# Second expert weights kept in SBUF, expert numbers read eight at a time, and row tables cleared at the start

## The chip, the cores and the metric

The kernel runs on one core of one Trainium2 chip, as one program. The metric is the time of the whole program on the device in microseconds (us): the median of several runs. The engines are TensorE (PE, with its weight loads PEld), VectorE (DVE), ScalarE (ACT), GpSimd (POOL) and SyncE (SP), which here does nothing but start transfers. Each engine works through its own list of instructions in order and waits on semaphores. All transfers share 16 DMA engines.

## The reference

The input is x of 8 batches, 512 tokens and 128 features, in fp32. Six steps add to it in turn:

```python
x = x + 0.5 * moe(layernorm(x))     # mixture of experts
x = x + attention(layernorm(x))     # 16 heads of 8, rotary, causal
x = x + 0.5 * moe(layernorm(x))     # the same weights again
x = x + 0.5 * fp6(layernorm(x))     # a 128x128 product on values rounded to 6 bits
x = x + mixer(layernorm(x))         # a gated scan over time and a gated FFN
x = x + 0.5 * fp6(layernorm(x))

def moe(x):                         # 8 experts, each token goes to 2 of them
    logits = x @ router_w + router_b
    scores, idx = top_k(logits, 2);  gates = softmax(scores)
    for expert e:                   # W1[e] 128x512, W2[e] 512x128
        out += c[e] * (relu(x @ W1[e] + b1[e]) @ W2[e] + b2[e])   # c[e]: gate, or 0
```

## The kernel before

**Planning.** The kernel is first written down as a graph of operations (`add`, class `Graph`): for each one its engine and estimated time, what it reads and writes, which buffers it takes, and operations that it must follow (`order`). `Graph.search` plays this through a model of the engines, of the DMA wire and of the buffer slots (`SLOTS`, `CAPS`), chooses an order and, where there is a choice, an engine, and the instructions are then issued in that order. Any changed cost, buffer or dependency therefore gives a new order of the whole program; priorities are the longest estimated way to the end plus a `skew`.

**Mixture of experts.** It runs in groups of batches: stage 0 has the groups of batches 0-1, 2-4 and 5-7, stage 2 (after the attention) has four groups of two. For a group, `moe_front` normalizes (rows `um`), computes logits, ranks every token within its two experts, and gets for each token two places in a table of rows in DRAM. Each expert has a whole number of 128-row tiles there, so a group of two batches has 23 tiles and one of three has 31; unused rows must hold zeros or other finite numbers. `eids` is one row of integers in SBUF: the expert of each tile. GpSimd then scatters the rows, 128 tokens with each indirect DMA, into `rows_in` (L783).

`moe_tiles` goes over pairs of tiles. SyncE, for each tile: reads the tile's expert number from `eids` into a register (L813, with a check of its bounds) and starts a transfer of that expert's whole block of weights into one of six `wx` slots (L814). The block, 1156 numbers for each of 128 partitions, holds W1 (512), W2 (512), b2 (128) and b1 (4). SyncE also loads the pair's rows `xs` (L824). PE turns them (L835), does four products with W1 (`hp`, L846), ACT or DVE adds b1 and clips (`hs`, L858), PE does four products with W2 (`yp`, L867; each product is two matmul instructions), DVE adds b2 (`yo`, L876), which frees the wx slot, and SyncE stores the pair to `rows_out` (L881). `moe_combine` gathers each token's two rows with indirect DMAs on GpSimd (L898) and adds them with their gates (L911).

**Clearing.** `clear_rows` (L467) fills a table with zeros from a tile of 128 x 128 zeros, repeated. There are four tables, one for each group number, used by both stages. Table 0 is cleared on SyncE behind the loads of x; the others are in the list `late`, each ordered behind the scatters of an earlier group. In the same list are the constants of the attention and of the tail (`load_late`): the rotary table, weights, biases, and so on. They were ordered behind the scatters of the second group. `clear_for_attention` has GpSimd clear buffers of the attention, and halve two bias vectors (L512 to L514).

**Attention and tail.** `attention` is a chain of `bursts` of score matmuls (L1018), with a pass over them on DVE (L1070), exponentials on ACT (L1081), a mask on GpSimd (L1089) and products with the values (L1125). Expert tiles of both stages are put between them by the planner. `fp6_weight` prepares the rounded weight, and `tail` does the last three steps for each batch.

Of the kernel before, what the change touches and what calls it, by code (L numbers as in the profile page):

```python
# [15 lines left out]
P = 128  # L16
# [22 lines left out]

E_W1, E_W2, E_B2, E_B1 = 0, NFC * P, 2 * NFC * P, 2 * NFC * P + P  # L40
E_ALL = E_B1 + NFC

SLOTS = {"ps": 8, "g": 34, "pm": 8, "wx": 6, "h": 9, "s": 20}
# [303 lines left out]
def kernel(  # L347
    ctx: ExitStack,
    tc: tile.TileContext,
    x: bass.AP,  # L350
    wexp: bass.AP,
    rw: bass.AP,
    rb: bass.AP,
# [51 lines left out]

    late = []

# [5 lines left out]

    def load_late(b, ap, bulk):
        late.append(lambda after: add(
            dma(0), lambda e: nc.sync.dma_start(out=b.t, in_=ap), w=[b], bulk=bulk, order=[after]))
        return b
# [3 lines left out]

    def const(name, ap, is_late=False):
        b = fixed(name, ap.shape)
        n = 4
        for d in ap.shape:
            n *= d
        return (load_late if is_late else load)(b, ap, n)

# [21 lines left out]
    mhalf = filled("mhalf", [P, GTX], -0.5)  # L450
    zero = filled("zero", [P, P], 0.0)
    ones = filled("ones", [P, P], 1.0)

    n_g = max(len(gs) for gs in GROUPS.values())
    n_0 = len(GROUPS[0])
    rows_in, rows_out = [], []
    for g in range(n_g):
        n = max(tiles_of(len(gs[g])) for gs in GROUPS.values() if g < len(gs)) * TW
        rows_in.append(Buf(None, None, "", dram.tile([n, P], F32, tag=f"rows_in{g}", name=f"rows_in{g}")))
        rows_out.append(Buf(None, None, "", dram.tile([n, P], F32, tag=f"rows_out{g}", name=f"rows_out{g}")))  # L460

    def clear_rows(g, order, skew=0.0):
        t = rows_in[g].t
        n = t.shape[0]
        return add(
            dma(0),
            lambda e: nc.sync.dma_start(  # L467
                out=t.rearrange("(n p) c -> p n c", p=P),
                in_=zero.t.unsqueeze(1).to_broadcast([P, n // P, P]),
            ),  # L470
            r=[zero], w=[rows_in[g]], bulk=n * P * 4, order=order, skew=skew,
        )

    for b in range(2, nb):
        load_x(b)
    sp.append(clear_rows(0, sp[-1:], 1e4))
    for g in range(1, n_g):
        late.append(lambda after, g=g: clear_rows(g, [groups[0, min(g, n_0) - 1]["sent"][-1]]))
    rope_s = const("rope_s", rope, True)
    wattn_s = const("wattn_s", wattn, True)  # L480
    future_s = const("future_s", future, True)
    vec_s = const("vec_s", vecs, True)
    wq8_s = const("wq8_s", wq8, True)
    wmix_s = const("wmix_s", wmix, True)
    wout_s = const("wout_s", wout, True)
    half_bq = fixed("half_bq", [P, P])
    load_late(half_bq, bq.partition_broadcast(P), P * P * 4)
    half_vec = fixed("half_vec", [P, 2])
# [5 lines left out]
    def clear_for_attention(after):  # L494
        for h in range(2):
            for k in range(2):
                t = nstat[h][k]
                add(pool(S, each=1e-3), lambda e, t=t: nc.gpsimd.memset(t.t, 0.0), w=[t], order=[after])
        for v in vpad:
            for q in range(4):  # L500
                part = v.t[:, 16 * q : 16 * q + 16, :]
                add(pool(S, each=1e-3), lambda e, part=part: nc.gpsimd.memset(part, 0.0),
                    w=[(v, ("clear", q))], order=[after])
            v5 = v.t.rearrange("p (a two) c -> p a two c", two=2)
            for k in range(2):
                at = 16 * k + DK
                add(pool(32, each=1e-3),
                    lambda e, v5=v5, k=k, at=at: nc.gpsimd.memset(v5[:, :, k, at : at + 1], 1.0),
                    w=[v], order=[after])

        def halves(e):
            nc.gpsimd.tensor_scalar_mul(half_bq.t, half_bq.t, 0.5)  # L512
            nc.gpsimd.tensor_scalar_mul(half_vec.t[:, 0:1], vec_s.t[:, V_BG : V_BG + 1], 0.5)
            nc.gpsimd.tensor_scalar_mul(half_vec.t[:, 1:2], vec_s.t[:, V_BD : V_BD + 1], 0.5)  # L514

        add(pool(P, k=2, each=1.3e-3), halves, r=[vec_s], w=[half_bq, half_vec], order=[after])
# [112 lines left out]
    def moe_front(s, g):  # L629
# [4 lines left out]
        n_b = len(bs)  # L634
        GT, NTL = n_b * NT, tiles_of(n_b)
        n8 = GT * NE
# [140 lines left out]
        for n in range(n_b):  # L777
            for k in range(2):
                for t in range(NT):
                    i = n * NT + t  # L780

                    def scatter(e, n=n, k=k, t=t, i=i):
                        ins = nc.gpsimd.indirect_dma_start(  # L783
                            out=rows_in[g].t[0 : NTL * TW, :],
                            out_offset=bass.IndirectOffsetOnAxis(ap=at(k)[:, i : i + 1], axis=0),
                            in_=tokens(us[n])[:, t, :], in_offset=None,
                            bounds_check=NTL * TW - 1, oob_is_err=False,
                        )
                        state["scattered"].append(unordered(ins, f"out{name}"))

                    state["sent"].append(add(
                        ("POOL", 1.02, 2.2, None), scatter, r=[us[n], (keep, f"at{k}"), (rows_in[g], ("s", name, i, k))],
                        bulk=P * P * 4,
                    ))

    def moe_tiles(s, g):

        NTL = tiles_of(len(GROUPS[s][g]))
        state = groups[s, g]
        for j in range((NTL + 1) // 2):  # L800
            tiles = [i for i in (2 * j, 2 * j + 1) if i < NTL]
            w = len(tiles)
# [6 lines left out]
            for i in tiles:  # L809
                wx[i] = buf("wx", "wx", f"wx_{name}")  # L810

                def fetch(e, i=i, wxi=wx[i]):
                    r = nc.sync.value_load(state["eids"].t[0:1, i : i + 1], min_val=0, max_val=NE - 1)  # L813
                    nc.sync.dma_start(  # L814
                        out=wxi.t, in_=wexp[bass.ds(r, 1), :, :].rearrange("o p c -> p (o c)")
                    )

                loads.append(add(
                    ("SP", 0.73, 3.0, None), fetch, r=[state["eids"]], w=[wx[i]], acq=[wx[i]],
                    bulk=P * E_ALL * 4, order=loads[-1:],  # L820
                ))

            def rows_of(e, xs=xs, rows=rows, halves=halves):
                ins = nc.sync.dma_start(  # L824
                    out=halves(xs.t), in_=rows_in[g].t[rows, :].rearrange("(h p) c -> p h c", p=P)
                )
                data_from(ins, state["scattered"])

            rows_loads.append(add(
                dma(0), rows_of, w=[xs], acq=[xs], deps=state["sent"], bulk=w * P * P * 4, order=rows_loads[-1:]  # L830
            ))

# [30 lines left out]
            for h, i in enumerate(tiles):  # L863

                def second(e, h=h, i=i, yp=yp, hs=hs, wx=wx):
                    for fc in range(NFC):
                        nc.tensor.matmul(  # L867
                            yp.t[:, ts(h, P)], hs[i].t[:, ts(fc, P)],
                            wx[i].t[:, E_W2 + fc * P : E_W2 + (fc + 1) * P],
                            start=(fc == 0), stop=(fc == NFC - 1),  # L870
                        )

                add(pe(P, NFC), second, r=[hs[i], wx[i]], w=[(yp, h)], acq=[yp, yo] if h == 0 else [])

# [5 lines left out]
            def store(e, yo=yo, rows=rows, halves=halves):  # L880
                state["stored"].append(nc.sync.dma_start(  # L881
                    out=rows_out[g].t[rows, :].rearrange("(h p) c -> p h c", p=P), in_=halves(yo.t)
                ))

            state["done"].append(add(dma(0), store, r=[yo], bulk=w * P * P * 4))

    def moe_combine(s, g):

        state = groups[s, g]
        NTL = tiles_of(len(GROUPS[s][g]))  # L890
        for n, b in enumerate(GROUPS[s][g]):
            for k in range(2):
                y = buf("g", "y", f"y{k}_{s}_{b}")
                for t in range(NT):
                    i = n * NT + t

                    def gather(e, y=y, k=k, t=t, i=i):
                        ins = nc.gpsimd.indirect_dma_start(  # L898
                            out=tokens(y)[:, t, :], out_offset=None,
                            in_=rows_out[g].t[0 : NTL * TW, :],  # L900
                            in_offset=bass.IndirectOffsetOnAxis(ap=state["at"](k)[:, i : i + 1], axis=0),
# [3 lines left out]

                    add(("POOL", 1.02, 2.2, None), gather, r=[(state["keep"], f"at{k}")], w=[(y, t)],
                        acq=[y] if t == 0 else [], deps=state["done"], bulk=P * P * 4)
# [452 lines left out]
    for g in range(n_0):  # L1360
        moe_front(0, g)
        if g + 1 < n_0:
            late.pop(0)(None)
    for go in late:
        go(groups[0, 1]["sent"][-1])
    clear_for_attention(groups[0, 0]["sent"][-1])
# [3 lines left out]
    bursts = attention()  # L1370
    fp6_weight(bursts[0])
    for g in range(len(GROUPS[2])):
# [91 lines left out]
```

## Time and profile before

| | |
|---|---|
| median of 3 runs | 1101.2 us (1100.86 to 1102.36) |
| profiled execution: its own time, its span | 1096.83 us, 1095.1 us |
| granted TensorE clock, mean | 0.932 |
| busy: PE, DVE, POOL, ACT | 929.3, 752.4, 536.1, 515.3 us |
| moved by DMA | 163.6 MB, of it wx 177 transfers of 578 KB |
| first scatter, first row load, first expert matmul | 28.57, 51.68, 55.11 us |
| the expert tiles' second matmuls, L867 | 1416 instructions, 199.1 us |

The profile is of one execution. The expert tiles of stage 0 begin at 55 us, alone at first and from about 180 us on between the bursts of the attention, which ends at about 757 us. The first weight load of stage 2 is issued at 488.8 us, and its last tile ends at about 935 us; from there on the tail is alone. In the rows, L numbers are lines of the kernel before. The groups of section 5 give busy time, mean duration and idle time before it; windows give busy times of each engine in a stretch. "issue" is time in which the engine waited for nothing that the profile shows.

### The profile page before, as it was taken

To read this page: it belongs to the slowest core of one execution; us is meant where nothing else is said; L and a number is where in the kernel's file an instruction comes from. 1 tells how busy PE (TensorE), PEld (TensorE's weight loads), DVE (VectorE), ACT (ScalarE), POOL (GpSimd) and SP (SyncE) were. 2 spreads that over 40 slices of the span, in tenths; PEclk is the share of its full clock that TensorE was granted. 3 is DMA by queue.
4 is the path that set the end of the run, shared out by engine and by line. 5 is a ranking of instruction groups with operands and counts; after the bars stand their busy time and mean duration, and the time that the engine had idled before them with its cause. 6 is when DMAs were issued, how large, how long until landed. Compare 5 with 4: busy or idle time off the path is not lost.

```text
span 1095.1 us, 22590 instructions
## 1 busy us (share of the span) xinstructions
PE 929.3 (85%) x7282; PEld 694.7 (63%) x7282; DVE 752.4 (69%) x2797; ACT 515.3 (47%) x1335; POOL 536.1 (49%) x681
## 2 busy tenths in 40 slices
PE   5357958799899989998999999998978989976873
PEld 5357946677667764554765776666877878535452
DVE  7501216278866579997786667966338859999996
ACT  3123523235465654555755665564435536543521
POOL 2771053525722168447246223784048654774552
PEclk9978968799999998999998999999989989988985
DMA  4737969487455411015233354233978876100001
GB/s 147 261 113 250 384 196 331 132 297 225 132 191 158 145 56 50 26 36 182 64 117 100 107 155 141 76 122 93 303 266 270 264 245 214 30 17 1 20 19 39
DMA packets 102070, 163.60 MB, mean 149 GB/s; under 512 B 11200, under 2 KB 70720, under 8 KB 101952
## 3 DMA queue, kind: packets, MB, share of 16 engines
q1 hardware_dynamic: 93760, 145.37, 41.1%
q0 software_dynamic: 8192, 16.79, 5.1%
q8 instruction: 58, 0.95, 0.3%
q14 instruction: 60, 0.49, 0.1%
HBM read 129.28 MB, written 29.16 MB: 145 GB/s over the span
## 4 chain that ended last, share of the span: by engine, by line
PE 50%; DVE 21%; issue 10%; POOL 8%; DMA 6%; another core or an unknown queue 2%; ACT 1%; SPq 1%; POOLq 0%; DVEq 0%; ACTq 0%
PE hp L846 11%; PE yp L867 10%; PE sb L1018 8%; PE sa L1018 7%; PE av L1125 5%; DMA wx<-in_wexp 3%; DVE sa L1070 3%; POOL y L898 3%; POOL rows_in L783 1%; PE xp L835 1%; PE lp L663 1%; DMA y<-rows_out,keep 1%; DVE q L1226 1%; DVE x L911 1%
## 5 line engine op out<-in xcount | busy, mean ns | idle before, releaser
L858 ACT ACTIVATE hs<-hp,wx 128x128 f32<-128x128 f32 x704 | 199.5, 372 | 231.0 <-PE hp L846 115.4
L1070 DVE CUSTOM_DVE_ANT_0 sa<-sa,future_s 128x384 f32<-128x384 f32 (+3 forms) x512 | 241.1, 514 | 86.6 <-PE sa L1018 50.8
L867 PE MATMUL yp<-wx,hs 128*128 128x128 f32 x1416 | 199.1, 287 | 56.3 <-issue 30.2
L1081 ACT ACTIVATE pm<-sb 128x512 f32<-128x512 f32 x320 | 173.3, 598 | 147.5 <-PE sb L1018 67.3
L867 PEld LDWEIGHTS yp<-wx,hs 128*128 128x128 f32 x1416 | 180.7, 200 | 67.8 <-issue 53.6
L846 PE MATMUL hp<-xt,wx 128*128 128x128 f32 x1416 | 200.5, 289 | 9.2 <-DMA wx<-in_wexp 5.1
L1018 PE MATMUL sb<-qa,ka 32*128 32x256 f32 (+3 forms) x1024 | 198.0, 467 | 10.3 <-DVE nstat L1070 6.8
L846 PEld LDWEIGHTS hp<-xt,wx 128*128 128x128 f32 x1416 | 183.1, 202 | 31.4 <-issue 11.8
L1089 POOL TENSOR_SCALAR_AFFINE_SELECT pm<-pm 128x256 f32<-128x256 f32 x256 | 104.3, 426 | 199.2 <-ACT pm L1081 196.6
L1018 PE MATMUL sa<-ka,qm 32*128 32x384 f32 (+3 forms) x1024 | 191.9, 474 | 4.2 <-DVE qm L537 2.4
L898 POOL DMA_INDIRECT y<-rows_out,keep x128 | 136.2, 1064 | 89.7 <-PE yp L867 47.9
L783 POOL DMA_INDIRECT rows_in<-um,keep x128 | 128.7, 1005 | 70.4 <-DVE route L751 32.9
L876 DVE TENSOR_TENSOR yo<-yp,wx 128x128 f32<-128x128 f32 x177 | 48.7, 285 | 124.1 <-PE yp L867 65.3
L1018 PEld LDWEIGHTS sb<-qa,ka 32*128 32x128 f32 x1024 | 98.3, 186 | 49.2 <-DVE nstat L1070 16.7
L1018 PEld LDWEIGHTS sa<-ka,qm 32*128 32x128 f32 x1024 | 88.3, 189 | 31.7 <-issue 7.9
L1125 PE MATMUL av<-pm,vpad 128*32 128x256 f32 (+3 forms) x1024 | 80.4, 445 | 1.8 <-POOL pm L1089 1.3
L535 DVE COPY xt<-xp 128x256 f32<-128x256 f32 (+1 forms) x83 | 33.8, 408 | 59.2 <-PE xp L835 27.4
L1070 DVE DVE_READ_ACCUMULATOR2_ANT nstat<- 128x1 f32 x512 | 72.0, 141 | 0.0
L1125 PEld LDWEIGHTS av<-pm,vpad 128*32 128x32 f32 x1024 | 28.7, 111 | 59.2 <-issue 41.1
L911 DVE SCALAR_TENSOR_TENSOR x<-y,keep,x 128x128 f32<-128x128 f32 x128 | 45.3, 368 | 20.6 <-DMA y<-rows_out,keep 18.6
L835 PE MATMUL xp<-cst,xs 128*128 128x128 f32 x177 | 36.3, 287 | 12.5 <-DMA xs<-rows_in 12.0
L835 PEld LDWEIGHTS xp<-cst,xs 128*128 128x128 f32 x177 | 22.6, 148 | 17.3 <-issue 14.6
(215 smaller groups left out, 1233.6 us busy)
## 6 DMA issues: line engine op xcount, KB each, us to landing
wx<-in_wexp SPq DMA_DIRECT2D x177, 578.0 KB
xs<-rows_in SPq DMA_DIRECT2D x85, 128.0 KB
rows_out<-yo SPq DMA_DIRECT2D x85, 128.0 KB
rows_in<-zero SPq DMA_DIRECT2D x2, 1984.0 KB
rows_in<-zero SPq DMA_DIRECT2D x2, 1472.0 KB
x<-in_x SPq DMA_DIRECT2D x8, 256.0 KB
rows_in<-um,keep POOLq DMA_INDIRECT x128
y<-rows_out,keep POOLq DMA_INDIRECT x128
```

Source lines behind the costliest of these rows:

```text
L783: ins = nc.gpsimd.indirect_dma_start(out=rows_in[g].t[0 : NTL * TW, :], out_offset=bass.IndirectOffsetOnAxis(ap=at(k)[:, i : i + 1], axis= ...
L835: nc.tensor.transpose(xp.t[:, ts(h, P)], halves(xs.t)[:, h, :], ident)
L846: nc.tensor.matmul(hp.t[:, ts(fc, P)], wx[i].t[:, E_W1 + fc * P : E_W1 + (fc + 1) * P], xt.t[:, ts(h, P)], start=True, stop=True,)
L858: nc.scalar.activation(o, a, AF.Relu, bias=bias)
L867: nc.tensor.matmul(yp.t[:, ts(h, P)], hs[i].t[:, ts(fc, P)], wx[i].t[:, E_W2 + fc * P : E_W2 + (fc + 1) * P], start=(fc == 0), stop=(fc == ...
L898: ins = nc.gpsimd.indirect_dma_start(out=tokens(y)[:, t, :], out_offset=None, in_=rows_out[g].t[0 : NTL * TW, :], in_offset=bass.IndirectO ...
L911: nc.vector.scalar_tensor_tensor(X[b].t[:, t, :], tokens(y)[:, t, :], state["gates"](k)[:, i : i + 1], X[b].t[:, t, :], ALU.mult, ALU.add,)
L1018: nc.tensor.matmul(sc.t[:, at : at + hi - lo], stat.t[rows, ts(m, P)], mov.t[rows, lo:hi], start=True, stop=True,)
L1070: nc.vector.tensor_tensor_reduce(out=sc.t[:, at : at + wd], in0=sc.t[:, at : at + wd], in1=future_s.t[:, S - wd : S], scale=-1.0, scalar=3 ...
L1081: nc.scalar.activation(pm.t[:, (h % 2) * S : (h % 2 + 1) * S], sc.t, AF.Exp, scale=scale)
L1089: nc.gpsimd.affine_select(out=diag, in_=diag, pattern=[[0, 2], [1, P]], compare_op=ALU.is_ge, fill=0.0, base=0, channel_multiplier=-1,)
L1125: nc.tensor.matmul(av.t[32 * j : 32 * j + 32, m * P :], v.t[:, row, :], pm.t[:, at : at + S - m * P], start=first, stop=last,)
```

## The change

1. **Weights.** W2 leaves the block `wexp`, whose rows now have 644 numbers. All eight experts' W2 come as one array `wsec` into a resident SBUF tile `w2_s` (128 x 4096 numbers), in two loads right behind the clears. The second matmuls take their right operand from `w2_s` at a place that a register of PE gives.
2. **Expert numbers.** Reads are for eight tiles at a time, without a check of bounds: SyncE reads them for its weight loads, and PE reads them too, for the places in `w2_s`. The planner is told 0.6 us for a read on SP, 0.3 on PE and 0.52 for a weight load (0.73 before). A read on PE comes after the fourth last second matmul before it.
3. **Tables.** Three tables instead of four: the last group of stage 2 uses table 0 again, with dependencies for it. All three are cleared at the start, from a tile of 128 x 1024 zeros that takes a slot of the attention's `pm` buffers, with longer runs.
4. **Constants.** `late` is split: what the attention needs is ordered behind the first group's scatters, what the tail needs (and the halving, and `fp6_weight`) behind a burst of the attention, number 20.

```diff
-E_W1, E_W2, E_B2, E_B1 = 0, NFC * P, 2 * NFC * P, 2 * NFC * P + P
+E_W1, E_B2, E_B1 = 0, NFC * P, NFC * P + P
 E_ALL = E_B1 + NFC
+W2 = NFC * P
+REGS = 8
...
-    zero = filled("zero", [P, P], 0.0)
...
+    table = lambda s, g: g if g < n_0 else 0
...
+    zero = buf("pm", "pm", "zero")
+    add(pool(2 * S, each=1e-3), lambda e: nc.gpsimd.memset(zero.t, 0.0), w=[zero], acq=[zero], skew=9e3)
+    for g in range(n_0):
         t = rows_in[g].t
         n = t.shape[0]
-        return add(
+        sp.append(add(
             dma(0),
-            lambda e: nc.sync.dma_start(
-                out=t.rearrange("(n p) c -> p n c", p=P),
-                in_=zero.t.unsqueeze(1).to_broadcast([P, n // P, P]),
+            lambda e, t=t, n=n: nc.sync.dma_start(
+                out=t.rearrange("(p n) c -> p (n c)", p=P).rearrange("p (q c) -> p q c", q=4),
+                in_=zero.t[:, 0 : n // 4].unsqueeze(1).to_broadcast([P, 4, n // 4]),
             ),
...
-    sp.append(clear_rows(0, sp[-1:], 1e4))
-    for g in range(1, n_g):
-        late.append(lambda after, g=g: clear_rows(g, [groups[0, min(g, n_0) - 1]["sent"][-1]]))
...
+    w2_s = fixed("w2_s", [P, NE * W2])
+    for q in range(2):
+        half = slice(q * NE * W2 // 2, (q + 1) * NE * W2 // 2)
+        load((w2_s, q), wsec[:, half], P * NE * W2 * 2, to=w2_s.t[:, half])
...
+        def registers(engine, to, at):
+            to.update(zip(at, nc.values_load_multi_w_load_instructions(
+                state["eids"].t[0:1, at[0] : at[-1] + 1], engines=[engine], min_val=0, max_val=NE - 1,
+                skip_runtime_bounds_check_because="the tile's expert is held below NE",
+            )[1]))
+
         for j in range((NTL + 1) // 2):
+            if (2 * j) % REGS == 0:
+                at = list(range(2 * j, min(2 * j + REGS, NTL)))
+                loads.append(add(
+                    ("SP", 0.6, 0.6, None), lambda e, at=at: registers(mybir.EngineType.SP, expert, at),
+                    r=[state["eids"]], order=loads[-1:],
+                ))
+                o = add(("PE", 0.3, 0.0, "F"), lambda e, at=at: registers(mybir.EngineType.PE, which, at),
+                        r=[state["eids"]], order=seconds[-4:-3])
+                ready.update({i: o for i in at})
...
-                    r = nc.sync.value_load(state["eids"].t[0:1, i : i + 1], min_val=0, max_val=NE - 1)
                     nc.sync.dma_start(
-                        out=wxi.t, in_=wexp[bass.ds(r, 1), :, :].rearrange("o p c -> p (o c)")
+                        out=wxi.t, in_=wexp[bass.ds(expert[i], 1), :, :].rearrange("o p c -> p (o c)")
                     )
...
                             yp.t[:, ts(h, P)], hs[i].t[:, ts(fc, P)],
-                            wx[i].t[:, E_W2 + fc * P : E_W2 + (fc + 1) * P],
+                            w2_s.t[:, bass.ds(which[i] * W2 + fc * P, P)],
...
+    for go in late["attention"]:
+        go(groups[0, 0]["sent"][-1])
...
-    fp6_weight(bursts[0])
+    for go in late["tail"]:
+        go(bursts[2 * HALF])
+    halve(bursts[2 * HALF])
+    fp6_weight(bursts[2 * HALF])
```

## The prediction

> **What bounds the kernel now.** I read the page first: busy shares, the slices, the chain that ended last.
>
> ```profile
> PE 929.3 (85%) x7282; PEld 694.7 (63%) x7282; DVE 752.4 (69%) x2797; ACT 515.3 (47%) x1335; POOL 536.1 (49%) x681
> ...
> PEclk9978968799999998999998999999989989988985
> DMA  4737969487455411015233354233978876100001
> ...
> PE 50%; DVE 21%; issue 10%; POOL 8%; DMA 6%; another core or an unknown queue 2%; ACT 1%; SPq 1%; POOLq 0%; DVEq 0%; ACTq 0%
> ```
>
> TensorE works 85% of the span, so the sum is made against its 166 us of idle time. DMA is 6% of the chain and SyncE 1% (11 us). DMA slices of 8 and 9 stand in expert stages only. Next, windows cut by stage; the first pair of numbers behind the window's length is PE's busy time, the last three are granted clock, DMA share and GB/s.
>
> ```profile
> 55.00:90.00 35.00, 16.98 (x102) 15.88 (x102) 2.13 (x7) 6.84 (x24) 24.85 (x29) 0.75 0.32 99
> 90.00:135.00 45.00, 42.91 (x364) 42.22 (x365) 11.01 (x37) 23.40 (x84) 0.89 (x1) 0.97 0.99 361
> 135.00:160.00 25.00, 11.70 (x69) 10.82 (x68) 2.08 (x8) 4.56 (x16) 15.11 (x16) 0.69 0.61 206
> 160.00:220.00 60.00, 50.04 (x299) 41.56 (x299) 26.07 (x91) 21.45 (x69) 24.42 (x28) 0.82 0.72 232
> ...
> 757.00:800.00 43.00, 37.84 (x327) 36.85 (x328) 20.16 (x84) 19.30 (x67) 5.03 (x5) 1.00 0.92 299
> ...
> 820.00:900.00 80.00, 70.09 (x513) 62.07 (x512) 59.33 (x207) 40.43 (x122) 54.47 (x50) 0.95 0.81 257
> ...
> 940.00:1095.00 155.00, 107.17 (x458) 69.74 (x458) 143.20 (x403) 58.47 (x126) 87.32 (x75) 0.83 0.06 21
> ```
>
> Two things are to be seen. Where DMA is full (90 to 135, 757 to 800) PE is nearly full too: 95% and 88%. Where PE is bad (55 to 90 at 49%, 135 to 160 at 47%) DMA is at 0.32 and 0.61 and GpSimd is busy 71% and 60%: bursts of scatters and gathers, at a granted clock of 0.75 and 0.69. From 940 on VectorE does 143 of 155 us and the change touches nothing. Third, the chain of waits inside 757 to 800, with the weight loads on it:
>
> ```profile
> 761.00 5.07 DMA wx<-in_wexp
> ...
> 769.65 5.42 DMA wx<-in_wexp
> ...
> 778.76 5.47 DMA wx<-in_wexp
> ...
> 787.57 6.35 DMA wx<-in_wexp
> ```
>
> That is 22.3 of 43 us on the chain, yet PE idles only 5.2 us there: it does other tiles while a load flies. Last, the two lines that read an expert's number and use it on SyncE (duration in ns, min/median/max):
>
> ```profile
> L813 SPq TENSOR_LOAD <-eid x177: 15/272/867, 27.0 to 918.7; - x177
> L813 SPq FUSED_REGOPS  x177: 13/152/181, 27.5 to 919.0; - x177
> L813 SPq SEQ_ASSERT  x177: 8/18/378, 27.7 to 919.2; - x177
> ```
>
> ```profile
> L814 SPq FUSED_REGOPS  x177: 3/37/705, 27.8 to 919.3; - x177
> L814 SPq MOVE wx<-in_wexp x177: 3/29/697, 27.9 to 919.4; - x177
> ```
>
> **The base.** The profiled execution took 1096.8 us (span 1095.1 and 1.7 around it), 4.4 under the median of 1101.2. The terms are differences and are set on the median. About 0.2% (2.2 us) is what a measurement of this kernel can tell from no change.
>
> **Part 1, second weights resident.** A tile's wx shrinks from 578 to 322 KB: 256 KB by 177 tiles is 46.4 MB less of 163.6, for 2 MB loaded once. At the 361 GB/s of 90 to 135 that is 129 us of wire time, but only PE's idle time beside a full wire can come back. Low end: PE sat 5.1 us, in 7 waits, directly behind wx. High end: all PE idle time in the three full stages, 45 - 42.91 = 2.1, 43 - 37.84 = 5.2 and 80 - 70.09 = 9.9, together 17.2. I take the first two whole and half of the third, where GpSimd also bursts (54 of 80 us): 12 us gained. What is late next is PE itself: a tile has 8 + 8 matmuls of L846 and L867, eight of which start within 0.89 us in the timeline (111 ns each), plus a turned half, about 1.9 us, as long as 720 KB of traffic takes at 361 GB/s (2.0 us).
>
> **Part 2, numbers read eight at once.** SyncE: L813 costs 272 + 152 + 18 = 442 ns a tile, 78 us in all. Now there are 23 reads (3 for each of five groups of 23 tiles, 4 for each of two of 31), with no check of bounds. The same thread issues row loads and stores, which thus wait less. At most the chain's 11 us of SyncE goes, at least nothing; I take 2 gained, since the queue waits 248 us for VectorE to free a weight slot, which the change leaves.
>
> TensorE gets two new things. Reads: 23, on the engine that is the bound, and what is queued behind a read are the matmuls of all stages, attention's too. No row shows a read on PE nor one of eight numbers. From SyncE's 272 ns, one read for a batch is 23 x 0.272 = 6.3 us, and a price for each number is 177 x 0.272 = 48. I take one price for a batch, half of it behind matmuls already queued: 3 lost. Zero is the end below; nothing in a read can gain. [...]
>
> Addresses: the right operand of L867 comes through a register, 4 places a tile, 708 in all. The nearest row is SyncE's 37 + 29 = 66 ns for one address: 46.7 us if PE waits for each, 0 if all are made ahead. Four addresses are 0.26 us against the 0.89 us in which the array does the tile's eight second matmuls, so I take them as hidden but for half of a tile's first: 177 x 0.033 = 6 lost. The cover is matmuls in the queue; without it the 46.7 stand. [...]
>
> **Part 3, tables cleared first.** Three tables (1472 + 2 x 1984 = 5440 KB) instead of four (6912). SyncE issues them and the two halves of the resident weights right behind the x loads: 5 issues instead of 1, about 2 us more on a thread that stands from 7.1 to 27.9. The wire is at a share of 0.19 from 12 to 28 us; 5.4 + 2 MB at 361 GB/s take 21 us, to about 33, then six loads of 322 KB to about 39. The first matmul waits for xs, which lands at 53.8 behind 16 scatters: 15 us of cover. The wide zero is one memset of 1.1 us (twice the 565 ns of L502) while GpSimd is idle to 6.1. All this is nothing on the path. What goes are two clears in mid-run (issued at 167.0 and 249.6), 5.6 and 4.2 us of wire ahead of row loads: between 0 and 9.8; PE is 94% and 100% busy in those 20 us windows, so I take 1 gained.
>
> The clear that held the third group's scatters is gone, so their 24 x 1.28 = 31 us may move from 184-209 into the 48 us (86 to 134) in which GpSimd is idle. Bounds: 10 gained (PE's idle time from 160 to 220), or PE runs at 49% as from 55 to 90 instead of 95%, 14 lost. I take 0. The tail's constants and their halving go into the attention; the first user is at 707 us, so nothing. Table 0 serves the first and the last group, some 500 us apart: nothing.
>
> **Sum.** -12 - 2 - 1 + 3 + 6 + 0 = -6: 1090.8 in the profile's terms, 1095 as a median.
>
> **Rivals.** Registers on PE decide (slower): reads and addresses stand in TensorE's order uncovered. The point is where a tile's extra PE time passes the idle time beside it; PE idles under 10% in the stages that matter. Half of 46.7 plus half of 48 is 47, plus nothing else; less the 15 gained, 1133; with one read price a batch and half the addresses, 1101 + 23 + 6 - 15 = 1115. I set it at 1118. For it: PE is 85% busy and every instruction on it delays all stages. Against it: 111 ns a matmul leaves room for 66 ns an address.
>
> Scatters meet full tiles (slower): the third group's burst falls under 90 to 135 and costs 14, the freed time of 160 to 220 is filled by waits for gathers: 1101 + 14 - 6 = 1109. For it: 49% against 95%. Against it: the planner may spread them.
>
> More comes back: 17 for the wire, 10 for the scatters, 3 for SyncE and the clears, 9 lost: 1080. For it: weight loads on the chain. Against it: PE's idle time hardly stands beside them.
>
> It does nothing: traffic was hidden anyway, gains of 9 meet losses of 9: 1101.
>
> **How the numbers follow.** Forecast (1088 to 1099) 0.38; more comes back 0.13; nothing 0.10; registers 0.25; scatters 0.14. Hence faster 0.50 (0.01 of the forecast's weight is within 0.2%), same 0.11, slower 0.39. The forecast's own range is 1088 to 1099; eight in ten need part of the cases of both signs: 1074 to 1124, left out the far half of the register case and the deep end of the gain.
>
> **What would show it.** Right: wx near 322 KB, DMA share from 90 to 135 and 757 to 800 near 0.6 with PE at 97%; the spacing of L867's matmuls still 111 ns; 23 reads on PE under 0.5 us. Wrong: gaps put down to "issue" or PE's queue ahead of the second matmuls; reads of 1.6 us or more; clears landing after 40 us; a new stretch at half PE under GpSimd's scatters between 86 and 134.

## The result, and the profile after

The changed kernel is slower: 1136.65 us in the median (1130.82 to 1139.28, 6 runs) against 1101.62 us (1096.33 to 1102.97, 6 runs) for the kernel before. The ratio is 1.0321, 95% interval 1.0287 to 1.0354, so +35 us where the prediction had -6. Times differ with the chip that a program ran on: the kernel before takes about 1102 us on some (called a slow chip below; this comparison is on one) and about 1021 us on others (a fast chip), so each ratio below is against the kernel before on the same chip. The profiled execution took 1134.79 us (span 1133.1). In the rows below, L numbers are lines of the changed kernel: `hp` is L870 (L846 before), `yp` L891 (L867), the reads of numbers L811, the weight load L838, the scatters L790, the gathers L923.

First the page of the changed kernel: busy times, granted clock and DMA share over 40 slices, and the chain that ended last.

```profile
PE 955.6 (84%) x7282; PEld 705.8 (62%) x7282; DVE 739.1 (65%) x2780; ACT 525.4 (46%) x1357; POOL 537.6 (47%) x682
...
PEclk9995989988999998889999999999975998799995
DMA  9541766732423310021222233314754771000001
...
PE 51%; DVE 19%; DMA 9%; issue 8%; another core or an unknown queue 5%; ACT 4%; POOL 3%; SPq 1%; POOLq 0%; DVEq 0%; ACTq 0%
```

The transfers did become lighter (117.82 MB instead of 163.60, each wx load 322 KB), and still DMA holds more of the chain, 9% instead of 6. PE has the same 7282 matmuls and only 26 us more of busy time. Now the windows that the prediction showed, of the changed kernel. PE's busy time is the first pair behind the length, VectorE's the third, GpSimd's the fifth.

```profile
55.00:90.00 35.00, 25.00 (x170) 22.80 (x171) 3.78 (x11) 11.40 (x40) 29.31 (x38) 0.92 0.46 137
90.00:135.00 45.00, 24.88 (x168) 22.98 (x169) 5.77 (x18) 12.32 (x44) 12.98 (x14) 0.69 0.45 131
135.00:160.00 25.00, 19.95 (x169) 19.07 (x168) 5.32 (x17) 8.79 (x32) 10.18 (x11) 0.98 0.68 190
160.00:220.00 60.00, 50.65 (x377) 47.97 (x377) 18.53 (x70) 28.15 (x98) 15.03 (x15) 0.89 0.69 189
757.00:800.00 43.00, 39.59 (x367) 33.01 (x367) 23.09 (x86) 22.00 (x66) 15.98 (x25) 1.00 0.48 129
820.00:900.00 80.00, 61.66 (x417) 57.18 (x418) 30.77 (x111) 26.95 (x96) 36.23 (x36) 0.79 0.58 161
```

The half-PE stretch that the prediction named as a wrong sign is there: 24.88 of 45 us from 90 to 135, where PE worked 95% before. But it is given back: the bad windows on both sides got better. The row to stop at is 820 to 900. VectorE does 30.77 us where it did 59.33. That work has to go somewhere, so the next windows are cut at the last gather of the last group, which starts at 974.0 us before and 980.2 after. First the kernel before, the stage ahead of it and the rest; then the changed kernel.

```profile
845.00:974.00 129.00, 116.91 (x756) 93.65 (x754) 108.08 (x371) 69.72 (x192) 82.11 (x74) 0.96 0.54 171
974.00:1095.10 121.10, 78.03 (x337) 53.03 (x336) 111.19 (x293) 38.11 (x82) 59.05 (x49) 0.78 0.05 19
```

```profile
860.00:980.20 120.20, 99.66 (x658) 83.15 (x658) 85.41 (x314) 60.41 (x179) 65.31 (x60) 0.87 0.49 137
980.20:1133.10 152.90, 114.59 (x502) 71.41 (x500) 141.06 (x400) 59.81 (x123) 71.22 (x59) 0.86 0.04 15
```

Here stand 31.8 of the 38.0 us between the two spans: behind the last gather VectorE has 400 instructions instead of 293, and the stretch is 152.9 us instead of 121.1. All are steps of the last three layers (the tail) that used to be placed between the expert tiles. The change edits none of these steps. Up to the last gather the changed kernel is only 6.2 us late: the attention's last score matmuls start 15.7 us later (763.3 instead of 747.6), and from there to the last gather, with less tail work between the tiles, it takes 9.5 less.

Last the new instructions, with duration in ns (min/median/max):

```profile
L811 SPq TENSOR_LOAD <-eid x23: 71/529/952, 26.5 to 917.3; - x23
L811 PEldq TENSOR_LOAD <-eid x23: 588/635/1146, 26.5 to 929.2; - x23
```

```profile
L891 PE MATMUL yp<-w_s,hs x1416: 269/275/582, 61.7 to 941.4; 128*128 x177
L891 PEldq FUSED_REGOPS  x708: 51/55/60, 59.3 to 940.0; - x177
```

A read of eight costs TensorE's queue 635 ns, an address 55 ns, four addresses a tile as predicted.

### The profile page after: what moved, and what is told of

The parts are those of the page before. It is cut to its first block, busy times and chain, and to the rows that moved or that the text cites. A ratio compares the mean times of both kernels' runs of the same rounds, so it can differ in the third digit from the quotient of the medians.

```text
span 1133.1 us, 22841 instructions
## 1 busy us (share of the span) xinstructions
PE 955.6 (84%) x7282; PEld 705.8 (62%) x7282; DVE 739.1 (65%) x2780; ACT 525.4 (46%) x1357; POOL 537.6 (47%) x682
## 2 busy tenths in 40 slices
DMA packets 90054, 117.82 MB, mean 104 GB/s; under 512 B 11216, under 2 KB 56912, under 8 KB 89680
## 4 chain that ended last, share of the span: by engine, by line
PE 51%; DVE 19%; DMA 9%; issue 8%; another core or an unknown queue 5%; ACT 4%; POOL 3%; SPq 1%; POOLq 0%; DVEq 0%; ACTq 0%
PE hp L870 12%; PE yp L891 11%; PE sb L1043 8%; PE sa L1043 6%; DMA wx<-in_wexp 6%; PE av L1150 5%; DVE sa L1095 3%; DMA y<-rows_out,keep 2%; PE xp L859 1%; PE lp L670 1%; DVE mix L1362 1%; ACT pm L1106 1%; POOL y L923 1%; PE gt L1356 1%
## 5 line engine op out<-in xcount | busy, mean ns | idle before, releaser
L882 ACT ACTIVATE hs<-hp,wx 128x128 f32<-128x128 f32 x692 | 195.1, 374 | 231.5 <-PE hp L870 106.0
L870 PE MATMUL hp<-xt,wx 128*128 128x128 f32 x1416 | 209.6, 294 | 46.5 <-DMA wx<-in_wexp 26.7
L870 PEld LDWEIGHTS hp<-xt,wx 128*128 128x128 f32 x1416 | 185.3, 204 | 64.4 <-issue 32.8
L891 PE MATMUL yp<-w_s,hs 128*128 x1416 | 198.3, 286 | 21.0 <-issue 18.5
L1043 PE MATMUL sb<-qa,ka 32*128 32x128 f32 (+3 forms) x1024 | 201.2, 476 | 9.7 <-ACT pm L1106 6.1
L1043 PE MATMUL sa<-ka,qm 32*128 32x384 f32 (+3 forms) x1024 | 194.3, 482 | 6.0 <-DVE nstat L1095 4.7
L891 PEld LDWEIGHTS yp<-w_s,hs 128*128 128x128 f32 x1416 | 181.5, 201 | 28.5 <-issue 24.4
L923 POOL DMA_INDIRECT y<-rows_out,keep x128 | 135.0, 1054 | 104.4 <-DMA wx<-in_wexp 66.0
L790 POOL DMA_INDIRECT rows_in<-um,keep x128 | 127.6, 997 | 38.2 <-issue 30.0
L1043 PEld LDWEIGHTS sb<-qa,ka 32*128 32x128 f32 x1024 | 100.8, 189 | 48.7 <-DVE nstat L1095 13.6
L1150 PE MATMUL av<-pm,vpad 128*32 128x256 f32 (+3 forms) x1024 | 83.6, 457 | 0.7 <-POOL pm L1114 0.5
```

Source lines behind the costliest of these rows:

```text
L790: ins = nc.gpsimd.indirect_dma_start(out=rows_in[tb].t[0 : NTL * TW, :], out_offset=bass.IndirectOffsetOnAxis(ap=at(k)[:, i : i + 1], axis=0),
L870: nc.tensor.matmul(hp.t[:, ts(fc, P)], wx[i].t[:, E_W1 + fc * P : E_W1 + (fc + 1) * P], xt.t[:, ts(h, P)], start=True, stop=True,)
L882: nc.scalar.activation(o, a, AF.Relu, bias=bias)
L891: nc.tensor.matmul(yp.t[:, ts(h, P)], hs[i].t[:, ts(fc, P)], w2_s.t[:, bass.ds(which[i] * W2 + fc * P, P)], start=(fc == 0), stop=(fc == N ...
L923: ins = nc.gpsimd.indirect_dma_start(out=tokens(y)[:, t, :], out_offset=None, in_=rows_out[tb].t[0 : NTL * TW, :], in_offset=bass.Indirect ...
L1043: nc.tensor.matmul(sc.t[:, at : at + hi - lo], stat.t[rows, ts(m, P)], mov.t[rows, lo:hi], start=True, stop=True,)
```

## The experiments

Three theories stood at the start. **Order theory:** the planner, given new costs, writes another order for the whole program, and that order costs the time. **Instruction theory:** TensorE's reads and addresses cost it (the prediction's first rival). **Table theory:** the clears and what they free cost it.

The figures of plans in the expectations are what the kernel's own planner computes for its order. The expectations in us for x1 to x4 were meant for a slow chip; to be set beside the results they are read as ratios to 1101.6 us.

**Old and new instructions in each other's order.** The planner's call is replaced by a fixed list of steps, with engine and buffer of each; the list is the one that the planner makes for the other kernel, with steps that only one kernel has put right before their first use.

```diff
-    order = G.search(bursts, SLOTS)
+    order = pinned(G)      # the other kernel's order
```

New instructions, old order (x1):

> All of the changed kernel's instructions (small weight blocks, resident second weights, register reads of eight on SyncE and TensorE, three tables cleared first), but every step put on the engine, at the place and in the buffer that the planner chose for the kernel before; the register reads stand right in front of their first use. Order theory (what costs 35 us is the new order that the planner makes from its changed costs): 1085 to 1102 us, no slower than before. Instruction theory (reads and addresses on TensorE cost it): 1125 to 1140, as the changed kernel. Table theory (clears first, shared table 0): 1115 to 1140 if it is the clears' transfers, 1100 if it is only what they let the planner do.

Old instructions, new order (x2):

> The reverse: full weight blocks of 578 KB, one read of the expert's number for each tile on SyncE, nothing on TensorE, in the order that the planner chose for the changed kernel; tables and clears as in the changed kernel. Order theory: 1130 to 1150 us, as slow as the changed kernel or slower, since 46 MB more have to pass in an order that was made for less. Instruction theory: 1095 to 1105. Table theory: 1125 to 1140.

Measured on a fast chip: x1 0.9907 (0.9873 to 0.9941), x2 1.0751 (1.0694 to 1.0807). Both stand with the order theory, for which x1 was expected at 0.985 to 1.000 and x2 at 1.026 to 1.044 or more: the same instructions gain 9.5 us in the old order, and the old ones lose 77 us in the new one without any instruction of part 1 or 2. The windows behind the last gather show the same fingerprint as the first two profiles, x1 first, then x2.

```profile
891.60:1012.60 121.00, 78.63 (x337) 53.12 (x336) 111.27 (x293) 38.10 (x82) 58.99 (x49) 0.79 0.05 19
```

```profile
944.70:1098.60 153.90, 114.06 (x501) 72.13 (x499) 141.63 (x403) 59.62 (x122) 71.45 (x59) 0.85 0.04 15
```

VectorE's 293 and about 400 instructions, 121 and 153 us, go with the order and not with the instructions. x2 shows one thing more, in its chain: full blocks in an order made for small ones wait for the wire, and DMA has 20% of the chain (9% in the changed kernel).

```profile
PE 43%; DVE 21%; DMA 20%; issue 5%; ACT 4%; POOL 4%; SPq 2%; POOLq 0%; DVEq 0%; ACTq 0%
```

**Single parts, each planned anew.** x3 is the kernel before with parts 1 and 2, x4 the kernel before with part 3.

> The kernel before with the resident second weights and the reads of eight, its four tables, clears and constants as they were; the planner makes its own order. Instruction theory: 1125 to 1140 us. Table theory: 1085 to 1100. Order theory: no fixed number, since it is a third order; near 1100 if the third group's scatters stay behind a clear in mid-run and that is what counts, up to 1140 if any new order is as bad.

> The kernel before with the third part of the change alone: three tables cleared first from the wide zero tile, constants loaded for the attention and for the tail apart; full weight blocks and one read for each tile. The planner makes its own order, with the third group's scatters free to move up. Table theory: 1120 to 1140 us. Instruction theory: 1095 to 1105. Order theory: 1110 to 1140 if the moved scatters are what costs.

On the fast chip x3 took 1.0378 (1.0322 to 1.0435), with 155.9 us behind the last gather; x4 1.0016 (0.9982 to 1.0049), with 121.5 us, though its third group's scatters run from 84 to 114 us instead of behind the first group's gathers. So the table theory falls, and the bad order comes with parts 1 and 2. The stretches of x3 and x4:

```profile
905.10:1061.00 155.90, 115.06 (x502) 73.45 (x500) 141.20 (x403) 57.56 (x119) 72.32 (x59) 0.84 0.04 15
```

```profile
902.10:1023.60 121.50, 77.29 (x337) 52.12 (x336) 111.45 (x293) 38.05 (x82) 59.00 (x49) 0.78 0.05 19
```

**One number of the planner.** Of what parts 1 and 2 tell the planner, the size of a weight load is the largest change. Two kernels change that number and no instruction; two more are the changed kernel itself and a neighbour of its order.

```diff
 # y2, in the changed kernel: what the planner is told of a load that moves 322 KB
-                    bulk=P * E_ALL * 4, order=loads[-1:],
+                    bulk=P * (E_ALL + W2) * 4, order=loads[-1:],
 # y3, in the kernel before: what it is told of a load that moves 578 KB
-                    bulk=P * E_ALL * 4, order=loads[-1:],
+                    bulk=P * (E_ALL - NFC * P) * 4, order=loads[-1:],
 # y4, in the changed kernel
-MIX = 0.2
+MIX = 0.25
```

> The changed kernel as it is, beside the kernel before on the chip of the other runs of this call (one kernel differed by some 80 us between two chips, so the comparison has to be made on one). Order theory: 1.03 to 1.05 of the time before, with the last gather some 155 us before the end as in its first profile, against 121 us in the kernel before. Instruction theory: the same ratio, but then the gap must not close in the two runs that change one number of the planner.

> The changed kernel with one number different: the planner is told that a weight load moves 578 KB, as before, while it moves 322. Its plan then ends the last gather 99 us before the end (126 in the changed kernel's plan), with 72 us of the last layer's VectorE work behind it (88). Order theory: 0.985 to 1.005 of the time before, last gather to end 120 to 125 us. Instruction theory: 1.03 or more, as the changed kernel, since every instruction is there.

> The kernel before with one number different: the planner is told that a weight load moves 322 KB, while it moves 578. No instruction is changed, only the order. Its plan has the last gather 127 us before the end and 89 us of the last layer's VectorE work behind it (98 and 70 before). Order theory: 1.04 to 1.08 of the time before, last gather to end about 155 us. Instruction theory and table theory: 1.00.

> The changed kernel with the planner's mixing of old and new priorities at 0.25 instead of 0.2: another order from the same costs, whose plan ends the last gather 126 us before the end too. If the loss comes from the costs that the planner is given: 1.03 to 1.06 of the time before, last gather to end about 155 us. If the loss is the luck of one order: anywhere from 0.98 to 1.06, and not tied to that stretch.

On one fast chip: y1 1.025 (1.0175 to 1.0325), y2 1.0004 (0.9969 to 1.0039), y3 1.061 (1.0539 to 1.0682), y4 1.0217 (1.0152 to 1.0283). Telling the old size takes the loss away with every new instruction in place; telling the new size to the kernel before makes it 6% slower with not one instruction changed. y4, a neighbouring order, is as bad, with 149.8 us behind the last gather. y1 and y4 both came out a little below the 1.03 expected at least. The stretches of y1, y2 and y3:

```profile
890.70:1045.00 154.30, 115.17 (x502) 72.92 (x500) 141.09 (x400) 59.94 (x123) 71.27 (x59) 0.87 0.04 15
```

```profile
894.10:1016.90 122.80, 82.73 (x347) 54.27 (x345) 112.07 (x304) 42.55 (x92) 60.33 (x50) 0.79 0.05 19
```

```profile
936.10:1086.40 150.30, 114.21 (x502) 71.58 (x500) 138.93 (x403) 59.95 (x127) 73.49 (x60) 0.87 0.04 16
```

The first numbers are to be read too: the last gather starts at 890.7 us in y1, 894.1 in y2, and 891.6 in x1. The plan of the changed kernel has it some 40 us earlier than the plan of before (808 instead of 849); on the chip the order that put 30 us of VectorE's work behind it was no earlier at all. y1 and y2 ran on one chip and reach it within 3.4 us of each other; from there on y1 takes 31.5 us longer.

**The terms of the sum, in the old order.** z1 is x1 without TensorE's reads and chosen addresses (each tile takes a fixed block, so its output is another one); z2 has full blocks, no resident tile and nothing on TensorE. p1 and p2 repeat z1 and x1 side by side, x5 repeats x1 alone.

```diff
 # z1 and p1, against x1
-                            w2_s.t[:, bass.ds(which[i] * W2 + fc * P, P)],
+                            w2_s.t[:, i % NE * W2 + fc * P : i % NE * W2 + (fc + 1) * P],
 # and the read on PE issues nothing; z2, against that
-                            w2_s.t[:, i % NE * W2 + fc * P : i % NE * W2 + (fc + 1) * P],
+                            wx[i].t[:, E_W2 + fc * P : E_W2 + (fc + 1) * P],
```

> The kernel of x1_new_ops_old_order (new instructions, old order) without TensorE's part of the numbers: no register reads on TensorE, and the second matmul takes the resident block of tile number modulo 8 at a fixed address instead of the chosen expert's (so its output is another one). It prices the two TensorE terms of the prediction, +3 and +6 us. If they are as predicted: 9 us faster than x1, ratio 0.982. If the address arithmetic is hidden and only the 23 reads show: 0.984 to 0.991. If TensorE's registers cost nothing: 0.991, as x1. [...]

> Old order, full weight blocks of 578 KB with the second weights in them, nothing on TensorE; from the change only SyncE's reads of eight, and the three tables cleared first. Against z1 it prices the wire term alone (-12 us predicted), against the kernel before SyncE's reads and the clears (-3 predicted). If the terms are right: 0.997 of before, z1 being 12 us faster. If the wire is worth nothing in this order: 0.98 to 0.99, equal to z1. If the wire is worth more: z2 at 1.00 and z1 at 0.975.

> The new instructions in the old order once more, as x1: 0.985 to 0.995 on any chip, if the sum of the prediction (-6 us) is right about the instructions. On a chip of the slow kind, against z1's 0.988 there: 0.991 if TensorE's reads and addresses cost the 2 to 3 us that x1 and z1 differ by, 0.997 if they cost the 9 predicted.

> z1 once more (old order, new instructions, without TensorE's reads and chosen addresses, the second matmul on a fixed block), now beside the full one on one chip. If the terms are as predicted (9 us): 0.8 per cent under the full one. If they are hidden: equal. If the difference between the calls was real (15 us): 1.3 per cent under.

> New instructions, old order, complete (as x1 and x5), beside p1. 0.99 of before on a chip of the fast kind, 0.99 to 1.00 on one of the slow kind; above p1 by 0 (hidden), 9 us (predicted) or 15 us (the difference between the calls).

All on slow chips: z2 0.9970 (0.9941 to 1.0000); z1 0.9884 (0.9848 to 0.9921), p1 0.9893 (0.9855 to 0.9931); x5 1.0019 (0.9979 to 1.0060), p2 1.0024 (0.9998 to 1.0050). Differences of ratios times 1102 us give the terms, with the half widths put together as a root of squares: SyncE's reads and the clears -3.3 us (0 to -6.5); the wire, z1 less z2, -9.5 (-4 to -15); TensorE's numbers, p2 less p1, +14 (+9 to +20). x5 and p2 lie above what was expected of them (at most 0.997 and 1.00 on a slow chip), which fits a last term larger than thought. The middle one can be seen in part in PE's idle time before the first matmuls (z2 first, then z1): the waits for wx go away, 4.3 us of them.

```profile
L861 PE MATMUL hp<-xt,wx 128*128 128x128 f32 x1416 | 202.1, 290 | 6.8 <-DMA wx<-in_wexp 4.3 <-ACT pm L1096 0.9 <-DVE route L684 0.7
```

```profile
L870 PE MATMUL hp<-xt,wx 128*128 128x128 f32 x1416 | 199.9, 288 | 2.8 <-issue 2.8
```

How TensorE's numbers cost 14 us is not settled. The middle spacing of the second matmuls is 112 ns in p1 and in p2 alike, and there is no gap ahead of a tile's first one that one has and the other has not (median 111 to 112 ns in both). The 23 reads fill 18 us of PE's queue in x5's profile, which is of the right size, yet where no indirect DMA runs they hold up no matmul. Set side by side matmul by matmul, p2's profile is 6.89 us behind p1's at 310 us and still 6.89 at 395 us, with two reads and 21 tiles' second matmuls in between; it is 3.30 behind at 611 and 3.29 at 684, with one read and 15 tiles. The lag, 8.5 us at the end of these two profiles, is built up where GpSimd issues indirect DMAs; how is open. No run kept the reads and left out the addresses. On a fast chip x1 was at 0.9907, so it may cost less there; that was not paired.

**How far the told size carries.** The size of y2, raised to 640 and 720 KB:

> The changed kernel's instructions, the planner told that a weight load moves 640 KB (it moves 322). The plan leaves 62.9 us of the last layer's VectorE work behind the last gather (88.5 in the changed kernel's plan, 71.6 when told 578). Order theory: last gather to end 110 to 118 us; 1005 to 1020 us against 1021 of before, if the stages ahead lose nothing. Instruction theory: 1.025, as the changed kernel. If told sizes only matter up to the true one: as y2, 1.00.

> As the last, told 720 KB: 51.7 us of the last layer's VectorE work behind the last gather in the plan. Order theory: last gather to end 95 to 110 us, and the tile stages ahead longer by part of that, since tiles now wait for tail work that the plan puts between them: 1000 to 1025 us. Instruction theory: 1.025.

On a slow chip 1.0014 (0.9983 to 1.0045) and 1.0020 (0.9989 to 1.0052). The stretch behind the last gather does become shorter, 109.1 and 99.9 us with 99.23 and 86.28 us of VectorE in it, but the last gather moves from 979.0 us (x5) to 991.0 and 1005.0. w1 misses its expectation of 1005 to 1020 on 1021 us (0.984 to 0.999), w2 is at the upper end of its own: past the old share, what is saved behind the last gather is lost ahead of it. Where, differs. In w1 the last score matmuls of the attention start 18.8 us later than in x5 (776.1 instead of 757.3), and from there to the last gather it is even 7 us quicker; in w2 they are 13.1 us late and the rest takes 12.9 us longer. That tail work between the tiles holds the tiles up can be the reason in w2 alone, and no run isolates it.

**The third group's scatters.** The kernels h1 to h3 hold them behind the first group's last gather, where they ran before. `moe_combine` returns its last gather, and the scatters of `moe_front` take it as `order`:

```diff
-    for g in range(n_0):
+    for g in range(n_0 - 1):
         moe_front(0, g)
...
-    for g in range(n_0):
+    moe_tiles(0, 0)
+    hold = moe_combine(0, 0)
+    moe_front(0, 2, [hold])
+    for g in range(1, n_0):
         moe_tiles(0, g)
```

> The changed kernel with the third group's scatters held behind the first group's last gather, as they ran in the kernel before; the planner is told the true size. If the moved scatters cost what the early tiles lost on the first chip: the 23rd tile's sum some 13 us earlier than in the changed kernel there, and 1.015 to 1.022 of the time before instead of 1.032 (on a chip of the fast kind, where the changed kernel's 23rd tile was only 3 us late: 1.02 as the changed kernel's 1.025). If what they lose early is given back where they used to run: 1.025 to 1.032. Last gather to end about 153 us in any case.

> The same, and the planner told 578 KB for a weight load. The plan leaves 70 us of the last layer's VectorE work behind the last gather, as in the kernel before. Order theory: 0.985 to 0.995 of before, as the new instructions in the old order, last gather to end 121 us. If the moved scatters don't matter: 1.00, as with the size told alone.

> The same with 640 KB told; 64.6 us of the last layer's VectorE work behind the last gather in the plan. Order theory: 0.98 to 0.995, last gather to end 112 to 118 us. If tail work ahead of the last gather holds the tiles up by as much as it saves behind: equal to the last.

On a slow chip h1 took 1.0351 (1.0310 to 1.0392). Its 23rd tile's sum starts at 121.0 us, where the changed kernel has 140.9 and the kernel before 127.8; yet the end is no better than the changed kernel's 1.0321, and the attention's last score matmuls start at 770.2 us, later than the changed kernel's 763.3. That fits scatters which give back where they used to run what they take from the early tiles; but h1 is also another order, and this is not taken apart. h2 took 0.9958 (0.9913 to 1.0004), h3 0.9938 (0.9887 to 0.9989), which is the one version with all new instructions that beats the kernel before on a slow chip, by 6.8 us, with its interval just clear of 1. As the best of seven such versions on slow chips, and with a median no better than h2's (1093.4 and 1092.8 us), that is weak. With 640 KB told, holding the scatters seems to help (0.9938 against w1's 1.0014); the two come from different chips and their intervals touch. Of the expectations, h1's 1.025 to 1.032 and h2's 0.985 to 0.995 were just missed, on the slow side.

**All orders together.** Twelve orders of the planner's own were run. The five that were told 322 KB (the changed kernel, x3, y3, y4, h1) took 1.022 to 1.061 of the time before, with 149 to 156 us from the last gather to the end. The seven told 578 KB or more (the kernel before, x4, y2, w1, w2, h2, h3) took 0.994 to 1.002, with 100 to 123 us. This, more than y4 alone, says that the loss goes with the told size and not with the luck of one order.

## Why the prediction was wrong, by its own steps

**The step that failed** is one sentence: "From 940 on VectorE does 143 of 155 us and the change touches nothing." The change edits nothing there, but the planner writes the tail's place into the order from the same costs that the change edits. Every term was worked out as if all steps stayed where they were. In the old order that gives +2.6 us on a slow chip (p2) and -9.5 on a fast one (x1), for the -6 of the sum; the new order adds 33 us to it on the slow kind (1.0321 - 1.0024) and 35 on the fast (1.0250 - 0.9907), each from two different chips of that kind. Without these 33 us the result would have stood near 1104: inside the range for eight in ten, 1074 to 1124, but above the forecast's own 1088 to 1099, because TensorE's term was too small (below).

**Why the planner misjudged it.** In its code a load holds the wire for its bytes divided by 330,000 a us, that is 1.79 us for 578 KB and 1.00 us for 322: 18 us saved in a group of 23 tiles. In the old order the last group's 23 tiles took 68.6 us with full blocks (z2) and 68.1 with small ones (z1), from one group's last sum to the next one's. Believing the tiles quick, it let them go first and the tail after them. y2 and y3 show that this one number makes the bad order; that its wire model is the reason is argued from the plan and these two profiles. It is not the whole of the misjudgment: the plan has the attention's last mask end 19 us earlier than the plan of before (655 instead of 674), and in the profiles it ends 15 us later (767.1 instead of 752.0). Why the stages up to there came out later was not looked into.

**Part 1, the wire:** -12 predicted, -9.5 (-4 to -15) measured in the old order, within the 5.1 to 17.2 given. That only PE's idle time beside a full wire can come back is borne out: matmul by matmul, z2's profile falls 2.0 us further behind z1's from 91 to 134 us and 3.1 from 757 to 803, two of the stretches that were named (2.1 and 5.2 us of idle time), and 0.1 from 310 to 396, within the attention. In the new order small blocks are worth far more (x2 1.075 against y1 1.025 on fast chips, about 50 us, with TensorE's numbers against them), since there the wire is on the path (DMA is 20% of x2's chain, 11% of y1's).

**Part 2, SyncE, and the clears:** -2 and -1 predicted, -3.3 together measured (0 to -6.5, so just short of clear). Reads of eight take SyncE 529 ns.

**Part 2, TensorE:** +9 predicted, +14 (+9 to +20) measured on slow chips: a second fault, a term mis-sized. The read was priced at 272 ns, SyncE's read of one number; eight numbers on TensorE took 635 ns in the median, over the 0.5 us named as the limit. That is 79 ns a number (635 / 8) and 18 us of the queue in all 23 reads, against 6.3 us at the price taken. How much of the 14 us is the reads and how much the addresses stays open. That four addresses a tile (55 ns each) pass beside the matmuls was the author's estimate; the matmul spacing of 112 ns with them (p2) and without (p1) agrees, and so does the lag that stays at 6.89 us over 21 tiles.

**Part 3, the scatters:** taken at 0, between -10 and +14, with no row for the middle; that it came out near 0 is in part luck. x4, part 3 alone with the scatters moved, says +1.6 us (-1.8 to +5.0) on a fast chip, and the changed kernel against h1 (1.0321 and 1.0351) says 0 within the intervals on slow ones, though both were planned anew. The stretch at half PE came as the rival described, and the windows on both sides of it gained. The prediction has these 24 scatters of the kernel before at 184 to 209 us; the last five of them follow at 220 to 229.

**The rivals.** Registers on PE was right in sign, but priced at 29 to 47 us against 14 measured, and not the cause: all the new instructions together make 2.6 of the 35 us lost (p2). Its condition, PE idle under 10% in the stages that matter, is not what the prediction's rows say: 12% from 757 to 800 and from 820 to 900. Scatters meet full tiles had its place right and its sum wrong. No rival had the order itself, although the chapter on the kernel says that any changed cost gives a new one.

**The signs.** DMA share from 757 to 800 fell to 0.48 (0.6 forecast) but PE there is at 92%, not 97; from 90 to 135, named with it, PE fell to 55%, which was one of the signs of being wrong. wx is 322 KB; the spacing of the second matmuls held (112 ns in the median, before and after). The reads on PE took 0.59 to 1.15 us in the changed kernel, at most 1.57 in x1 and 1.51 in p2: above the 0.5 us of the right sign, below the 1.6 us of the wrong one, a mark that no run gave.

## What to carry to other kernels

Where a planner or scheduler places the work from estimated costs, a change of a cost is a change of the whole order, and the untouched parts are the first place to look: compare what each engine still has to do behind a fixed event (here the last gather) in both plans and both profiles. Price the instructions by running them in the old order, and the order by running the old instructions in the new one. A resource that the model calls freed should be told to the planner only as far as the chip gives it back: here the old, larger size gave the better order (y2 1.0004, y1 1.025 of the time before on one chip).

## What the runs showed of the hardware

The two kinds of chip are the largest effect of the study: x1 and x5 are one and the same program and take 1011.2 and 1101.6 us. The difference lies where GpSimd issues indirect DMAs. Matmul by matmul, x5's profile lags x1's by 0.3 us at 35 us, by 23.6 when the second group's scatters are over and by 59.5 at 307 us. It stays at 59.5 until 392 us, where no indirect DMA is issued, and the lag goes from 73.5 to 73.0 between 759 and 803 us, where weight loads run but no indirect DMA. The windows over the second group's scatters (54 to 85) and the first group's gathers, x1 on a fast chip first, then x5 on a slow one:

```profile
54.00:85.00 31.00, 30.33 (x253) 29.95 (x253) 7.34 (x23) 16.12 (x58) 24.42 (x29) 1.00 0.78 227
107.00:128.00 21.00, 21.00 (x190) 21.00 (x189) 9.24 (x36) 12.03 (x45) 15.87 (x16) 1.00 0.96 287
```

```profile
54.00:85.00 31.00, 15.74 (x98) 14.53 (x97) 2.28 (x6) 5.68 (x20) 24.44 (x30) 0.73 0.30 89
131.00:152.00 21.00, 7.35 (x63) 6.95 (x61) 1.92 (x6) 3.66 (x13) 15.87 (x16) 0.80 0.55 160
```

GpSimd is as busy on both (24.4 and 15.87 us), but PE works 98% and 100% beside it on the one and 51% and 35% on the other, with the wire emptier too (DMA share 0.30 and 0.55 instead of 0.78 and 0.96). The prediction took PE's bad stretches under scatters and gathers for a property of the program; in x1, on a fast chip, they are not there. What the slow kind lacks was not found, nor whether it is the chip itself or its condition at the time: each chip stands in one set of runs only.
